# First keys on ScalarE's DMA queue, and a new order of two batches' normalisations in block 0 of a cross-attention and FFN kernel

## The chip, the cores and the metric

The kernel runs on one NeuronCore of one Trainium2 chip. The metric is the device time of one execution in microseconds (us). A core has five instruction streams that run beside each other and meet only through semaphores: TensorE (PE, matrix products; its weight loads are listed as PEld), VectorE (DVE), ScalarE (ACT), GpSimd (POOL) and SyncE (SP), which here only issues DMAs. ACT and POOL can issue DMAs as well. Each stream handles its instructions in the order of the program.

## The reference

Eight sequences of 256 tokens with 256 features go through one block. LayerNorm here has no learned parameters.

```python
x = x + softmax(mask(layernorm(x) @ ctx.T / 16)) @ ctx      # causal and key padding masks
h = silu((layernorm(x) @ w1.T) * w1_s) * ((layernorm(x) @ w2.T) * w2_s)
h = gelu((h @ h1.T) * h1_s)                                 # 1024 x 1024, ternary weights
h = gelu((h @ h2.T) * h2_s)
x = x + (h @ w3.T) * w3_s
```

## The kernel before

Two sequences make a block (`NB` = 2, 512 tokens, four tiles of 128 tokens), and there are four blocks, worked on in two pairs. For a pair, `pair` runs the FFN; its two wide layers use sums and differences of operand blocks in place of some products, and nearly all of the matmuls are there (L824). Operands are split into a high and a low part (`hyt` and `lyt`, `oh` and `ol`). The attention of later blocks is put between the FFN's steps by a plan written by hand (`stages_at`). The order of every engine's instructions is that in which the Python code emits them; no scheduler reorders them.

Only the attention of **block 0** runs with nothing beside it, as the prologue of the kernel. It is cut into two groups of one sequence each (`groups(0)` is `((0,), (1,))`), here called the first and the second batch; tiles 0 and 1 belong to the first, 2 and 3 to the second. `attention` holds one generator `stages` per batch and lets each go to its next `yield` in turn, so the two batches alternate stage by stage:

- `load_block` (L109) issues the DMAs. For block 0: mi, the mask row, on ACT's queue (L120); x as four tiles on SP (L123); the keys kt of the first and of the second batch on SP (L126); the values vs on SP (L129). Behind these SP issues the scales sc and s3 (L186, L188).
- Warm-up matmuls on zeros follow on PE (`keep_warm`, L161), then constants on POOL, and a load of ACT's square-root table (L184).
- `queries_turned` (L405), first stage: `sums` (L257) issues for each tile of the batch a statistics instruction (L261) and an aggregate (L262) on DVE. After the first batch's, DVE makes the mask row `row16` (L411). `masks_first` puts the masks into the score banks with bf16 matmuls (L370, L377); the L377 matmuls read `row16`.
- Second stage: `normed` (L278) issues the square root on ACT (L269, `root`), the reciprocal on DVE (L275, `turned_over`), and for each tile one `tensor_scalar` on DVE (L283, `scaled`) that gives the normalised tile of `ya`. Behind the second batch's, POOL copies one column (L419, `passed`), which holds back the weight loads behind it on POOL's queue (L148) until x is through.
- Third stage: four transposes for each batch on PE (`turned`, L301, tiles `pqt`), copied as `qt` by ACT for the first batch (L426) and by DVE for the second (L428). ACT then loads its exponential table (L339).
- Scores on PE (`ps`, L470), row maxima on DVE (L492), exponentials on ACT (L500), transposes (`pp`, L513), copies and reciprocals on DVE (L517 to L524), values on PE (`pv`, L537).
- The residual sum: one `scalar_tensor_tensor` on DVE for each tile (L551), which writes the tile of x again. For the first batch its accumulator gives the sums from which ACT makes the second LayerNorm's centre and root (L566 to L576). For the second batch `sums` follows. The list `held` carries a closure, `begun` (L578), from the first batch to the second's `sums`: it issues the first batch's reciprocal on DVE (L580) and the scaling of its tile 0 on POOL (L584). Tile 1 is scaled by DVE afterwards.
- Then, for the second batch, root, table load for the FFN's Silu (L339), reciprocal and two scalings; on PE the transposes of x (`pxt`), five warm-up matmuls (L161), and the transposes of `yf` (`pyt`). DVE casts the first batch's result and half of the second's to the high part `hyt` (L608), ACT casts the other half (L610), DVE makes the low part (L313). The first FFN matmuls are at L890.

Of the kernel before, what the change touches and what calls it, by code (L numbers as in the profile page):

```python
# [43 lines left out]
P = 128  # L44
B, S, D, H = 8, 256, 256, 1024
NB = 2
NT = NB * S // P
# [27 lines left out]
def _network(ctx, tc, g, exact, flag):  # L75
    nc = tc.nc
# [19 lines left out]
    def new(p, shape, tag, name, dt=F32, **kw):  # L96
        return p.tile(shape, dt, tag=tag, name=f"{v}{name}", **kw)

    def groups(t):

        return ((0,), (1,)) if t == 0 else ((0, 1),)

    def tokens(js):
        return slice(js[0] * S, (js[-1] + 1) * S)

    def tiles(js):
        return slice(2 * js[0], 2 * js[-1] + 2)

    def load_block(t, behind=None):  # L109

        xs = new(io, [P, NT, D], "xs", f"xs_{t}", bufs=2)
        kt = new(io, [P, NB, ND, S], "kt", f"kt_{t}", bufs=2)
        vs = new(io, [P, NT, D], "vs", f"vs_{t}", bufs=2)
        mi = new(io, [P if t else 1, TB], "mi", f"mi_{t}", I32)
        span = bass.ts(t, TB)
        if behind is not None:
            for tile_ in (xs[:, 0, :1], kt[:, 0, 0, :1], vs[:, 0, :1], mi[:, :1]):
                behind.memset(tile_, 0)
        if t == 0:
            nc.scalar.dma_start(out=mi, in_=g.mask[:, span])  # L120
        step = NT if t else 1
        for i in range(0, NT, step):
            nc.sync.dma_start(out=xs[:, i : i + step, :], in_=g.x[t, :, i : i + step, :])  # L123
        for n, js in enumerate(groups(t)):
            own = slice(js[0], js[-1] + 1)
            nc.sync.dma_start(out=kt[:, own], in_=g.ctx_t[t, :, own])  # L126
            if n == 0 and t:
                nc.sync.dma_start(out=mi, in_=g.mask[:, span].to_broadcast([P, TB]))
        nc.sync.dma_start(out=vs, in_=g.ctx_n[t])  # L129
        return xs, kt, vs, mi  # L130
# [11 lines left out]
    def load_weight(w, name):  # L142
# [7 lines left out]
        return chunks  # L150

    loaded = {0: load_block(0)}

    zeros = None if exact else new(work, [P, 2 * RAW], "raw", "zeros", BF16, bufs=3)
# [99 lines left out]
        yield  # L254
        yield nc.values_load(flag[0:1, 0:1], min_val=0, max_val=P * (LOW + len(wide) * RAW))

    def sums(src, js, mv, name, between=()):  # L257

        stats = new(tiny, [P, NT, nc.vector.BN_STATS_DIM], "stats", f"st{name}", bufs=2)
        for i in range(NT)[tiles(js)]:  # L260
            nc.vector.bn_stats(out=stats[:, i, :], in_=src[:, i, :])  # L261
            nc.vector.bn_aggr(out=mv[:, :, i], in_=stats[:, i, :])  # L262
            while between:
                between.pop()()

    def root(js, mv, name):
        own = tiles(js)
        std = new(tiny, [P, NT], "std", f"sd{name}", bufs=2)
        nc.scalar.activation(std[:, own], mv[:, 1, own], AF.Sqrt, bias=eps)  # L269
        return std  # L270

    def turned_over(js, std, name):
        own = tiles(js)
        rstd = new(tiny, [P, NT], "rstd", f"rs{name}", bufs=2)
        nc.vector.reciprocal(rstd[:, own], std[:, own])  # L275
        return rstd

    def normed(src, js, mv, y, name):  # L278
        scaled(src, range(NT)[tiles(js)], mv, turned_over(js, root(js, mv, name), name), y)

    def scaled(src, own, mv, rstd, y, engine=nc.vector):
        for i in own:
            engine.tensor_scalar(  # L283
                y[:, i, :],
                src[:, i, :],
                mv[:, 0, i : i + 1],
                rstd[:, i : i + 1],
                ALU.subtract,
                ALU.mult,
            )  # L290
# [45 lines left out]
    def table(t, js, func):  # L336

        if t == 0 and js == groups(t)[0 if func == AF.Exp else -1]:
            nc.scalar.activation(junk, eps, func)  # L339
# [65 lines left out]
    def queries_turned(t, js, once, xs, mi, pss):  # L405

        cols = tokens(js)
        mva = once("mva", "mva", [P, nc.vector.BN_AGGR_DIM, NT], tiny, bufs=2)
        sums(xs, js, mva, f"a_{t}_{js[0]}")
        if t == 0 and js == groups(t)[0]:  # L410
            nc.vector.tensor_scalar(row16[:, :TB], mi, 0.0, NEG, ALU.is_equal, ALU.mult)  # L411
        if not t:
            masks_first(js, pss)
        yield
        y = once("y", "ya", [P, NT, D])
        normed(xs, js, mva, y, f"a_{t}_{js[0]}")
        if t == 0 and js == groups(t)[-1]:
            passed = new(const, [P, 1], "passed", "passed")
            nc.gpsimd.tensor_copy(passed, y[:, NT - 1, :1])  # L419
        yield  # L420
        bias = mask_bias(t, js, once, mi)
        qt = once("qt", "qt", [P, ND, TB])
        for c, pt in turned(y, js, f"pqt_{t}_{js[0]}", *(() if t else (ps_mm, "mm"))):

            if t or js == groups(t)[0]:
                nc.scalar.activation(qt[:, c, cols], pt, AF.Copy, scale=1.0 / 16.0)  # L426
            else:
                nc.vector.tensor_scalar(qt[:, c, cols], pt, 1.0 / 16.0, None, ALU.mult)  # L428
        table(t, js, AF.Exp)
        yield  # L430
        return qt, bias, None
# [25 lines left out]
    def stages(t, js, once, result, xs, kt, vs, mi):  # L457
# [62 lines left out]
        own = slice(js[0], js[-1] + 1)  # L520
# [5 lines left out]
        for j in js:  # L526
            if t:
                pv = ps_at.tile([P, 2, D], F32, tag="at", name=f"{v}pv_{t}_{j}")
                pvs = [pv[:, h, :] for h in range(2)]
            else:  # L530

                p, tag = (ps_at, "at") if j else (ps_mm, "mm")
                pvs = [p.tile([P, D], F32, tag=tag, name=f"{v}pv_0_{j}_{h}") for h in range(2)]
            for h, (a, e) in enumerate(SPANS):
                n = (e - a) // P
                for k in range(n):
                    nc.tensor.matmul(  # L537
                        pvs[h],
                        lhsT=prt[:, j, bass.ds(a + k * P, P)],
                        rhs=vs[:, 2 * j + k, :],  # L540
                        start=(k == 0),
                        stop=(k == n - 1),
                    )

            first_ = len(groups(t)) > 1 and js == groups(t)[0]
            if first_:
                total, centre, squares, std = (
                    new(const, [P, 2], n, n) for n in ("total", "centre", "squares", "std0")
                )
            for h in range(2):  # L550
                nc.vector.scalar_tensor_tensor(  # L551
                    xs[:, 2 * j + h, :],
                    pvs[h],
                    rden[:, j, h : h + 1],
                    xs[:, 2 * j + h, :],
                    ALU.mult,
                    ALU.add,
                    **(dict(accum_out=total[:, h : h + 1]) if first_ else {}),
                )
        if t:  # L560
            yield
        mvf = once("mvf", "mvf", [P, nc.vector.BN_AGGR_DIM, NT], tiny)
        if first_:
            y = once("y", "yf", [P, NT, D])
            for i in range(2):
                nc.scalar.activation(  # L566
                    centre[:, i : i + 1], total[:, i : i + 1], AF.Copy, scale=-1.0 / D
                )
                nc.scalar.activation(
                    y[:, i, :],  # L570
                    xs[:, i, :],
                    AF.Square,
                    bias=centre[:, i : i + 1],
                    accum_out=squares[:, i : i + 1],
                )
            nc.scalar.activation(std, squares, AF.Sqrt, bias=eps, scale=1.0 / D)  # L576

            def begun():  # L578

                nc.vector.reciprocal(std, std)  # L580
                shifted(0, nc.gpsimd)

            def shifted(i, engine):
                engine.tensor_scalar(  # L584
                    y[:, i, :],
                    xs[:, i, :],
                    centre[:, i : i + 1],
                    std[:, i : i + 1],
                    ALU.add,
                    ALU.mult,  # L590
                )

            held.append(begun)
        else:
            sums(xs, js, mvf, f"f_{t}_{js[0]}", held)
        yield
        xst = once("xst", "xst", [P, ND, TB])
        yt = []
# [27 lines left out]
        if near(t):  # L626
            y = once("y", "yf", [P, NT, D])
# [19 lines left out]
        else:  # L647
# [5 lines left out]
            mean, rstd = on_all(mvf, ("row", "row2"), f"mf_{t}")  # L653
# [3 lines left out]
            y = once("y", "yf", [P, ND, TB])  # L657
# [600 lines left out]
```

## Time and profile before

| What | Value |
|---|---|
| Median of three timed runs | 349.14 us (347.75 to 349.73) |
| The profiled execution | 347.43 us |
| Its span, first to last instruction | 345.6 us |
| Mean granted TensorE clock | 0.995 |
| x's first tile, DMA issue to landing (chain) | 0.73 to 3.15 us |
| DVE's first statistics | 3.18 us |
| First score matmul (ps) | 7.84 us |
| First FFN matmul (L890) | 18.69 us |
| x (512 KB in four), keys (512 KB in two), values (512 KB) of block 0 | all issued by SP, 0.73 to 3.97 us |

The profile is that of one execution. A busy share says how long an engine had an instruction in hand. The chain that ended last is followed back from the last instruction: at each step to what released it, or to the instruction before it on its engine. A group in the timeline or the chain has its start, its duration, the engine, the line of the code, and how many instructions were merged; what stands in brackets is the time that the engine had been idle before it and what ended that.

### The profile page before, as it was taken

The page shows a single profiled execution, that of the slowest core. Times are in us where ns is not written, and L with a number is a line of the kernel's source. Part 1 is how long each engine was busy: PE and PEld are TensorE (multiplying, and loading weights), DVE is VectorE, ACT ScalarE, POOL GpSimd, SP SyncE. Part 2 cuts the span into 40 slices and gives each one's busy share as a digit, 9 for nine tenths or more (in the row PEclk, how much of TensorE's full clock was granted, in tenths as well). Part 3 has the DMA queues.
Part 4 walks back from the last instruction along what each step waited for, and adds up shares of the span by engine and source line. Part 5 has one row for each costly group of instructions (what it writes and reads, how often), then busy time and mean ns, then how long its engine had stood idle before and what let it go on. Part 6 is the DMA issues. An engine that isn't in the chain of part 4 may idle for free.

```text
span 345.6 us, 4329 instructions
## 1 busy us (share of the span) xinstructions
PE 334.0 (97%) x1508; PEld 269.9 (78%) x1508; DVE 270.3 (78%) x411; ACT 216.4 (63%) x301; POOL 36.6 (11%) x78
## 2 busy tenths in 40 slices
PE   8999999999999999999999999999999999999991
PEld 4777887877888888887888788886788887888781
DVE  5779876999799848686997875889948987856761
ACT  4866833358855854858671675356896686767620
POOL 3610000210002300030000003000010000000000
PEclk9999999999999999999999999999999999999998
DMA  5999972997596642579517474960635579530032
GB/s 184 342 297 273 294 256 82 358 280 252 151 399 228 197 146 99 164 251 326 204 47 246 127 251 127 292 248 2 243 123 182 173 250 353 201 121 0 0 123 70
DMA packets 20702, 68.81 MB, mean 199 GB/s; under 512 B 2465, under 2 KB 5313, under 8 KB 17090
## 3 DMA queue, kind: packets, MB, share of 16 engines
q0 software_dynamic: 7488, 36.70, 33.0%
q1 hardware_dynamic: 13040, 31.63, 27.2%
q8 instruction: 14, 0.23, 0.3%
q14 instruction: 14, 0.11, 0.1%
q10 hardware_dynamic: 146, 0.13, 0.1%
HBM read 55.86 MB, written 8.40 MB: 186 GB/s over the span
## 4 chain that ended last, share of the span: by engine, by line
PE 79%; DVE 8%; DMA 5%; ACT 3%; issue 2%; POOL 1%; DVEq 0%; POOLq 0%; ACTq 0%; SPq 0%
PE px_u L824 29%; PE px_y L824 15%; PE po L1112 8%; PE p L824 7%; PE pa L684 5%; PE pb L684 5%; PE ps L470 3%; PE pv L537 3%; DMA raw<-h2q 3%; DMA raw<-h1q 1%; DVE sign L218 1%; DVE ol L313 1%; PE pqt L301 1%; ACT oh L807 1%; DVE sta L261 1%
## 5 line engine op out<-in xcount | busy, mean ns | idle before, releaser
L824 PE MATMUL px_u<-oh,a 128*128 128x512 f32 x256 | 71.7, 395 | 1.1 <-ACT oh L807 0.8
L824 PE MATMUL px_u<-ol,a 128*128 128x512 f32 x256 | 70.8, 391 | 0.0
L824 PEld LDWEIGHTS px_u<-ol,a 128*128 128x128 f32 x256 | 47.9, 188 | 11.6 <-DVE ol L313 1.5
L824 PEld LDWEIGHTS px_u<-oh,a 128*128 128x128 f32 x256 | 47.5, 188 | 11.8 <-ACT oh L807 1.2
L697 ACT ACTIVATE gate<-pa,sc 128x512 f32<-128x512 f32 x32 | 21.6, 686 | 24.5 <-PE pa L684 22.1
L824 PE MATMUL px_y<-oh,a 128*128 128x512 f32 x128 | 34.5, 391 | 0.0
L824 PE MATMUL px_y<-ol,a 128*128 128x512 f32 x128 | 34.2, 389 | 0.0
L824 PEld LDWEIGHTS px_y<-ol,a 128*128 128x128 f32 x128 | 24.0, 188 | 5.0
L824 PEld LDWEIGHTS px_y<-oh,a 128*128 128x128 f32 x128 | 23.9, 188 | 5.0
L216 ACT ACTIVATE sign<-raw 128x1024 bf16<-128x1024 f32 x16 | 16.9, 1055 | 9.5 <-DMA raw<-h2q 4.1
L768 POOL DMA_DIRECT2D a<-S x16 | 8.5, 534 | 131.6 <-PE px_u L824 55.5
L218 DVE SCALAR_TENSOR_TENSOR sign<-raw,sign 128x1024 bf16<-128x1024 f32 x16 | 19.3, 1219 | 2.7 <-ACT sign L216 2.7
L684 PE MATMUL pa<-hyt,w 128*128 128x512 f32 x60 | 19.1, 399 | 0.2 <-DVE na L855 0.2
L684 PE MATMUL pb<-hyt,w 128*128 128x512 f32 x60 | 18.6, 391 | 0.2 <-DVE res L711 0.2
L684 PE MATMUL pa<-lyt,w 128*128 128x512 f32 x60 | 18.5, 390 | 0.0
L684 PE MATMUL pb<-lyt,w 128*128 128x512 f32 x60 | 18.5, 389 | 0.0
L852 ACT ACTIVATE nd<-nd,sc 128x512 f32<-128x512 f32 x16 | 10.7, 715 | 11.7 <-DVE nd L855 11.7
L824 PE MATMUL p<-oh,a 128*128 128x512 f32 x64 | 17.4, 394 | 0.4 <-DVE na L855 0.4
L313 DVE TENSOR_TENSOR ol<-nT,oh 128x1024 fp32r<-128x1024 f32 x12 | 14.5, 1222 | 3.6 <-ACT oh L807 3.6
L824 PE MATMUL p<-ol,a 128*128 128x512 f32 x64 | 17.1, 389 | 0.0
L855 DVE TENSOR_TENSOR na<-p,na 128x512 f32<-128x512 f32 x16 | 10.9, 688 | 7.9 <-PE p L824 7.9
L852 ACT ACTIVATE nb<-nb,sc 128x512 f32<-128x512 f32 x16 | 10.7, 717 | 10.0 <-DVE nb L855 10.0
(196 smaller groups left out, 651.1 us busy)
## 6 DMA issues: line engine op xcount, KB each, us to landing
a<-S POOLq DMA_DIRECT2D x16, 1024.0 KB, 5.1
a<-h1q POOLq DMA_DIRECT2D x6, 1024.0 KB, 7.8
a<-h2q POOLq DMA_DIRECT2D x6, 1024.0 KB, 5.1
raw<-h1q SPq DMA_DIRECT2D x8, 512.0 KB, 4.3
raw<-h2q SPq DMA_DIRECT2D x8, 512.0 KB, 5.9
vs<-ctx_n SPq DMA_DIRECT2D x4, 512.0 KB, 7.5
q<-h1q POOLq DMA_DIRECT2D x4, 512.0 KB, 20.1
q<-h2q POOLq DMA_DIRECT2D x8, 256.0 KB, 14.0
```

What stands on the lines that cost most here:

```text
L216: nc.scalar.activation(sign, raw, AF.Sign)
L218: nc.vector.scalar_tensor_tensor(sign, raw, 1.0, sign, ALU.mult, ALU.not_equal, accum_out=count[:, n : n + 1])
L313: nc.vector.tensor_tensor(lo, value, hi.bitcast(F32), ALU.subtract)
L470: nc.tensor.matmul(pss[j][h], lhsT=qt[:, c, bass.ts(2 * j + h, P)], rhs=kt[:, j, c, : e - a], start=(c == 0 and t > 0), stop=(c == ND - 1) ...
L537: nc.tensor.matmul(pvs[h], lhsT=prt[:, j, bass.ds(a + k * P, P)], rhs=vs[:, 2 * j + k, :], start=(k == 0), stop=(k == n - 1),)
L684: nc.tensor.matmul(pm, lhsT=wc[:, bass.ts(o, P)], rhs=x, start=(n == 0), stop=(n == len(steps) - 1),)
L697: nc.scalar.activation(gate, pa, AF.Silu, scale=sc[:, 0, o : o + 1])
L768: nc.gpsimd.dma_start(out=a, in_=src)
L824: nc.tensor.matmul(bank, lhsT=a[:, k, bass.ts(o, P)], rhs=x[k // 2][part][:, k % 2, :], start=start and (part, k) == steps[0], stop=stop a ...
L852: nc.scalar.activation(out, src, AF.Gelu, scale=sc[:, n, o : o + 1])
L855: nc.vector.tensor_tensor(out, one, other, ALU.add)
L1112: nc.tensor.matmul(po, lhsT=w3[j * QK + k][:, bass.ts(o, P)], rhs=xs_[j][k // 2][part][:, k % 2, :], start=(j == 0 and (part, k) == STEPS[0]),
```

## The change

Three edits, which touch block 0 and the functions that it shares with block 1. Nothing is computed differently, apart from one scaling that another engine does.

1. The first batch's keys are issued on ACT's DMA queue behind mi, instead of on SP's behind x.
2. The first batch's first normalisation is put into the closure list `held`, and the second batch's `sums` runs it ahead of the statistics of tile 3. Its tile 0 is scaled by POOL, its tile 1 by DVE.
3. `sums` takes a function `ahead`, called before each tile's statistics, and it now runs the closures in `held` before the second tile's statistics instead of after the first tile's aggregate. For the second batch the residual sums of x (L551) are no longer issued both at once but one ahead of each tile's statistics.

For block 1, whose `sums` call of the first normalisation now also gets `held`, that list is empty. The instructions on DVE change their order, not their number; the same goes for SP but for one DMA that moves to ACT, and POOL has one scaling more, DVE one less, in block 0.

```diff
             own = slice(js[0], js[-1] + 1)
-            nc.sync.dma_start(out=kt[:, own], in_=g.ctx_t[t, :, own])
+            queue = nc.sync if t or n else nc.scalar
+            queue.dma_start(out=kt[:, own], in_=g.ctx_t[t, :, own])
...
-    def sums(src, js, mv, name, between=()):
+    def sums(src, js, mv, name, between=(), ahead=None):
         stats = new(tiny, [P, NT, nc.vector.BN_STATS_DIM], "stats", f"st{name}", bufs=2)
-        for i in range(NT)[tiles(js)]:
+        for n, i in enumerate(range(NT)[tiles(js)]):
+            if ahead is not None:
+                ahead(n)
+            while n and between:
+                between.pop()()
             nc.vector.bn_stats(out=stats[:, i, :], in_=src[:, i, :])
             nc.vector.bn_aggr(out=mv[:, :, i], in_=stats[:, i, :])
-            while between:
-                between.pop()()
...
-        sums(xs, js, mva, f"a_{t}_{js[0]}")
-        if t == 0 and js == groups(t)[0]:
+        sums(xs, js, mva, f"a_{t}_{js[0]}", held)
+        y = once("y", "ya", [P, NT, D])
+        very_first = t == 0 and js == groups(t)[0]
+        if very_first:
+            def begun():
+                rstd = turned_over(js, root(js, mva, "a_0_0"), "a_0_0")
+                scaled(xs, (0,), mva, rstd, y, nc.gpsimd)
+                scaled(xs, (1,), mva, rstd, y)
+            held.append(begun)
             nc.vector.tensor_scalar(row16[:, :TB], mi, 0.0, NEG, ALU.is_equal, ALU.mult)
         if not t:
             masks_first(js, pss)
         yield
-        y = once("y", "ya", [P, NT, D])
-        normed(xs, js, mva, y, f"a_{t}_{js[0]}")
+        if not very_first:
+            normed(xs, js, mva, y, f"a_{t}_{js[0]}")
...
-            for h in range(2):
+            def added(h, j=j, pvs=pvs):
                 nc.vector.scalar_tensor_tensor(
                     xs[:, 2 * j + h, :],
...
+            if t or first_:
+                added(0)
+                added(1)
...
-            sums(xs, js, mvf, f"f_{t}_{js[0]}", held)
+            sums(xs, js, mvf, f"f_{t}_{js[0]}", held, None if t else added)
```

## The prediction

> **What bounds the kernel now.** I read the page first, for who is busy and when.
>
> ```profile
> span 345.6 us, 4329 instructions
> PE 334.0 (97%) x1508; PEld 269.9 (78%) x1508; DVE 270.3 (78%) x411; ACT 216.4 (63%) x301; POOL 36.6 (11%) x78
> ```
>
> TensorE (PE) is busy for 334.0 of 345.6 us. Busy time by stretch shows where the missing 11.6 us lie: PE works for 16.34 of the first 18.6 us and for 317.66 of the last 327.0 (2.26 and 9.34 us idle). After 18.6 us matmuls run with short waits, and none of the edits is there: their instructions all belong to block 0's attention, which is over by 19 us, and the later waits shift along with the run. So the change can only move the moment at which the long run of matmuls begins, and whatever that moves goes through to the end one for one. The whole stake is the prologue, and of it only its serial chain. So I read the chain that ended last, cut to the first 32 us (start, duration, what).
>
> ```profile
> 0.73 2.42 DMA xs<-x
> ...
> 5.54 0.18 DVE mva L262
> ...
> 7.22 0.78 PE pqt L301 x4
> 8.00 2.74 PE ps L470 x16
> ...
> 12.28 2.61 PE pv L537 x12
> ...
> 16.57 0.29 ACT sdf L269
> ...
> 16.88 1.28 ACT L339
> ...
> 18.28 0.36 ACT hyt L610
> ...
> 18.69 0.76 PE pa L890 x2
> ```
>
> The reader is to see a relay without slack: x lands, VectorE (DVE) makes the statistics, PE transposes, scores run (ps), softmax, values (pv), the sums of the second batch, a square root, a table load on ScalarE (ACT), one cast, and the first FFN matmul at 18.69. The timeline adds what stands beside the relay.
>
> ```profile
> 4.38 0.30 ACT L269 ACTIVATE sda<-mva,eps 128x2 f32<-128x2 f32 x1 [1.60 <-DVE mva L262]
> ...
> 6.66 0.74 DVE L283 TENSOR_SCALAR ya<-xs,mva,rsa 128x256 f32<-128x256 f32 x2
> ...
> 15.94 1.24 PE L161 MATMUL warm<-zeros 128*128 128x512 bf16 x5
> 16.19 0.55 POOL L584 TENSOR_SCALAR yf<-xs,centre,std 128x256 f32<-128x256 f32 x1 [2.76 <-issue]
> 16.45 0.43 DVE L584 TENSOR_SCALAR yf<-xs,centre,std 128x256 f32<-128x256 f32 x1
> ...
> 17.02 1.42 PE L301 MATMUL pyt<-ident,yf 128*128 128x128 f32 x8
> ...
> 17.75 1.15 DVE L608 CAST hyt<-pyt 128x512 fp32r<-128x512 f32 x2
> ```
>
> **Part 1, first normalisation.** Nothing is removed; one of four L283 operations goes to GpSimd (POOL), and the first batch's reciprocal and its tile 1 go ahead of the statistics of tile 3. DVE's pitches, from the rows: 0.43 from statistics to aggregate, 0.10 to the next instruction, 0.17 from reciprocal to scaling, 0.33 from scaling on. Tile 2's aggregate starts at 5.02 as before; the square root is ready (4.38 + 0.30 = 4.68). So reciprocal 5.12, tile 1 at 5.29 to 5.70, statistics of tile 3 at 5.62 instead of 5.12, aggregate 6.05 to 6.23, ACT's root 6.27 to 6.56, second reciprocal 6.59, then (0.20 behind a reciprocal that waited, as at 16.90 to 17.10) tile 2 at 6.79 and tile 3 from 7.12 to 7.53. Before, tile 3 was done at 6.66 + 0.74 = 7.40. The **first batch gains**: POOL, 0.2 behind the reciprocal as at L584, takes 0.55 and ends at 6.0, four transposes need 0.84 (7.19 to 8.03), so ACT can copy at 6.9 instead of 7.19. The **second batch loses** 0.13.
>
> Which of them counts? PE issues in program order, and both batches' transposes stand ahead of the first score. Before, the first score started at 7.84, when both had just ended together: ACT's copy at 7.19 + 0.60 = 7.79, and the last transpose, issued some 0.3 after tile 3's scaling. With the change the copy is 0.3 early, the transposes 0.13 late: the score starts 0.13 late. The early copy brings the table load behind it forward, but the exponentials after the first wait for DVE's maxima, which wait for PE's scores. So this part costs **+0.13**, bounds 0 (the second reciprocal waits less than I take) and +0.3 (VectorE slowed beside GpSimd). Behind POOL's new instruction stand the marker copy (L419) and the weight loads; that copy waited for tile 3 already, so they move by the 0.13. W2 is needed only at about 19 us and landed 7.8 after an issue near 9.
>
> Does GpSimd beside VectorE cost? At L584 both scale tiles at once: 0.55 and 0.43, where L283 alone takes 0.41. I take 0.02. The Trainium skill's page "SBUF — State Buffer", section "Who interferes with whom", speaks against this: a GpSimd operation and a VectorE `tensor_scalar` in a 2-port mode hold a shared port pair exclusively, and the later one blocks entirely. By it VectorE at 16.45 would have stood until 16.74, which the row does not show. If it held in the new place, GpSimd would end at some 6.25; that is still ahead of the second batch, so the sum would be the same.
>
> **Part 2, keys on ACT's queue.** ACT's issue of mi takes 0.52 (0.73 to 1.25); the first keys follow for some 0.45, so ACT's table load (1.29, 1.28 long) ends near 3.0 instead of 2.57. It is hidden: the first root is wanted at 4.38. On SP the second keys, vs, sc and s3 go 0.45 earlier. Nobody waits for them: keys landed 3.7 after an issue at 2.59 to 3.05, before 7, and the score wants them at 7.84. So the move **gains nothing**. What it can lose is x. Until now SP issued four x tiles ahead of all keys, one per 0.45 (four in 1.81); tile 0 landed at 3.15, so tiles 1 to 3 by that pitch at 3.60, 4.05 and 4.50. From now on 256 KB of keys enter the same 16 engines with tile 1. Three answers of the DMA view, cut to 5 to 6.5, 14.8 to 16.0 and 17.8 to 19.8 us (queue: packets, MB, share of engines):
>
> ```profile
> q1 hardware_dynamic: 217, 0.51, 99.1%
> ```
> ```profile
> q1 hardware_dynamic: 58, 0.24, 53.0%
> q0 software_dynamic: 58, 0.22, 51.3%
> ```
> ```profile
> q0 software_dynamic: 67, 0.53, 65.9%
> q1 hardware_dynamic: 71, 0.29, 38.3%
> ```
>
> The first says that 16 full engines move 340 GB/s of such packets, so the keys take 256 / 340 = 0.77 us of all engines. The others say that two queues share by packets, not bytes: 58 to 58, 67 to 71, and the queue with the bigger packets gets more bytes. Keys have packets twice as long as x's 1 KB, so x gets a third while both are pending. From 2.0 to 4.4 the engines are 77% busy; in some 1.2 us of contention that leaves 0.28 free. Tile 1 is then late by 0.77 - 0.28, say 0.5: 4.10 instead of 3.60, and its statistics start at 4.13 instead of 3.74. That is **+0.4** on the relay. Later tiles have more slack: tile 2 at 4.55 is wanted at 4.96, tile 3 later still. Bounds: 0 (tile 1's packets all get in first), and 0.8 (tile 0 is hit by all of the keys' time too). No row shows ACT and SP loading together, so I take the middle, nearest to the shared-queue rows.
>
> **Part 3, second batch's x and statistics.** Before: add, add, statistics, aggregate, reciprocal, statistics, aggregate. Now the first statistics go between the adds. Pitches: add to next 0.40, statistics to aggregate 0.45, then 0.10. First add 14.05, statistics 14.45, aggregate 14.90, second add 15.00 instead of 14.91 (its pv ended at 14.88), first batch's reciprocal at 15.49 (ACT's std ends at 15.46) instead of 15.86, statistics 15.54 instead of 15.91, the root at 16.20 instead of 16.57. So **0.37 is won at the root**, and ACT's table load and its cast could follow. But the second add is 0.09 late; it feeds four transposes, behind which, in PE's order, stand five warm-up matmuls and then the yf transposes, which started at 17.02 straight after the last warm-up. They start at 17.11 now. Four of them (0.11 apart, the last 0.27 long) end at 17.71, and DVE's first cast, which had waited for DVE itself until 17.75, now waits for them until 17.75. Its two casts end at 18.43 and 18.90 as before. The first FFN matmul waits for the first of them and for ACT: 18.49 instead of 18.69; the second waits for the second cast, and its weights load at 18.95, as before. **What is late next is VectorE's casts**, and the gain ends there: 0, bounds -0.37 and +0.09.
>
> **Sum.** 0.13 + 0.4 + 0 = +0.53 us on a profiled run of 347.43 (345.6 of span): 347.96. That run is 1.71 under the median of the three timed runs, 349.14 (347.75 to 349.73); the difference goes onto the median: **349.7 us**, +0.15%. Under 0.5% (1.75 us) is about what a measurement of this kernel can't tell from no change, so I forecast **no change**.
>
> **The rivals.**
> - *The new order pays.* Keys slip past x, and Part 3 keeps its 0.37: 0.13 - 0.37 = -0.24, 348.9. For it: 23% of engine time is free while x loads. Against it: L608 has no slack, and warm-up matmuls stand before pyt.
> - *Keys hit x in full.* Tile 0 and tile 1 wait out the whole 0.77: 0.8 + 0.13 + 0.09 = +1.0, 350.2. For it: a transfer lands when its slowest engine does. Against it: the keys enter some 0.5 behind tile 0.
> - *Slower, by PE's pace.* The first warm-up matmuls are 0.43 apart (2.44, 2.87, 3.29), the five later ones some 0.22 (1.24 for five); the pace doubled by 4.67, just as the row-mask matmuls began. Those wait for DVE's L411, which part 2 makes 0.4 late. If that hole keeps PE slow for one more block of work, the scores cost their 2.74 twice: +2.74 + 0.53, 352.4. It decides from the hole being long enough to undo the warm-up. Against it: at 11.84 PE had sat idle for 0.63 before L513's transposes without slowing. The Trainium skill's "TensorE: Matmul & The Clock Gate", Part 1, puts the idle time needed at about 3.4 us; by it this rival is worth nothing.
> - *The change does nothing visible*: each edit hidden, 349.1. It is the forecast without contention, and I count it there.
>
> **How the numbers follow.** Forecast, hidden edits included, 0.60; the order pays 0.18; keys in full 0.14; pace 0.08. Single runs of the kernel before spread by 1 us either side, so a median of a few can stray by as much. Range: 348.9 - 1.0 = 347.9 to 350.2 + 1.0 = 351.2; the pace case and some straying stay outside. Slower by over 0.5% (above 350.9): the pace's 0.08, and straying from the forecast (0.09) and from keys in full (0.04): 0.21. Faster by over 0.5% (below 347.4): straying from the first rival and the forecast, 0.08. Between: 0.71.
>
> **What would show it.** In the profile after: tile 1's statistics waiting for x's DMA past 3.8; the first score at 8.2 to 8.5 (7.84 before), of which 0.13 remain if x is on time; the root some 0.37 earlier against pv's end than the 1.69 of before, and yet the second FFN matmul's weights no earlier against it. I am wrong if tile 1 is on time, if the L608 casts move forward with the root, or if matmuls of the scores are twice as far apart.

## The result and the profile after

| | before | after |
|---|---|---|
| Median of 22 runs each, taken in turns on one chip | 347.61 us (345.73 to 349.73) | 348.93 us (346.71 to 350.57) |
| Ratio, with its 95% interval | | 1.0053 (1.0036 to 1.0070) |
| The profiled execution, and its span | 347.43, 345.6 | 349.05, 347.2 |
| Statistics of tile 1, of tile 2 start | 3.74, 4.57 | 5.29, 6.16 |
| First score matmul starts | 7.84 | 9.87 |
| The 16 score matmuls (ps) take | 2.89 | 4.15 |
| First weight load of the FFN | 18.69 | 21.90 |

The changed kernel is **slower**: by the ratio 1.84 us (1.25 to 2.43), or 0.53%, with an interval that leaves out no change; the two medians are 1.32 apart, which lies in that interval. The lines below, from the page of the changed kernel, show that TensorE (PE) has hardly more to do; the time is one of waiting and of pace.

```profile
span 347.2 us, 4330 instructions
PE 335.0 (96%) x1507; PEld 271.4 (78%) x1508; DVE 270.3 (78%) x410; ACT 216.8 (62%) x301; POOL 37.9 (11%) x79
```

The chain that ended last, cut to the first 32 us (start, duration, what):

```profile
1.18 4.09 DMA xs<-x
5.29 0.44 DVE sta L268
...
6.94 1.37 POOL ya L288
8.36 1.72 PE pqt L306 x8
10.08 3.96 PE ps L485 x16
...
19.59 0.29 ACT sdf L274
...
21.93 0.78 PE pa L910 x2
```

Before, this chain began with x's first tile (0.73, 2.42 long) and had the scores at 2.74. Now it begins with a **later tile of x, 4.09 us** on its way, goes over a GpSimd (POOL) scaling that was not there, and the same 16 score matmuls take 3.96. The timeline of the changed kernel (in brackets the idle time before, and what ended it) says who waited:

```profile
5.29 0.43 DVE L268 BATCH_NORM_STATS2 sta<-xs 128x6 f32<-128x256 f32 x1 [1.50 <-DMA xs<-x]
...
6.29 0.21 PE L382 MATMUL ps<-row 1*128 1x128 bf16 x1 [0.98 <-DVE row L426]
...
6.94 1.36 POOL L288 TENSOR_SCALAR ya<-xs,mva,rsa 128x256 f32<-128x256 f32 x1 [4.07 <-DVE rsa L280]
```

VectorE (DVE) stood 1.50 us for x; behind it the mask row was late, and PE stood 0.98 us before its row-mask matmuls.

**Where the 3.21 us at the FFN's start come from** (21.90 - 18.69), by these rows: 1.59 are there when tile 2's statistics start; 0.44 more come up to the first score (9.87 against 7.84 is 2.03), where GpSimd's scaling lies; the scores take 1.26 longer; and the rest of the way is 0.08 shorter. **Where they go:** the profiled spans differ by 1.6 only. The stretch behind the FFN's start is 325.3 us long here and 326.9 before. Over the twelve profiles of the experiments it is 325.5 to 326.8, in no order by the size of the prologue, so it has a scatter of its own of some 1.5 us, and these two profiles lie at its ends. A small part of it can be named. In the chain of the kernel before, cut to 277 to 296 us, stands a DMA; behind it and two steps on ACT, PE stood idle for 0.30 us, up to 290.72:

```profile
279.39 9.23 DMA raw<-h2q
```

The rest stays open. In the same cut, the chain of the changed kernel has matmuls alone:

```profile
276.95 19.27 PE px_u L844 x85
```

So the timed ratio, not the two spans, is the measure of the change.

### The profile page after: what moved, and what is told of

Same layout as the page of the kernel before. It is cut to its first block, busy times and chain, and to the rows that moved or that the text cites. A ratio compares the mean times of both kernels' runs of the same rounds, so it can differ in the third digit from the quotient of the medians.

```text
span 347.2 us, 4330 instructions
## 1 busy us (share of the span) xinstructions
PE 335.0 (96%) x1507; PEld 271.4 (78%) x1508; DVE 270.3 (78%) x410; ACT 216.8 (62%) x301; POOL 37.9 (11%) x79
## 4 chain that ended last, share of the span: by engine, by line
PE 84%; DVE 7%; ACT 3%; DMA 2%; issue 2%; POOL 1%; SPq 0%; POOLq 0%; DVEq 0%; ACTq 0%
PE px_u L844 34%; PE px_y L844 15%; PE po L1132 8%; PE p L844 7%; PE pa L704 5%; PE pb L704 5%; PE ps L485 3%; PE pv L552 3%; DMA raw<-h1q 1%; DMA xs<-x 1%; DVE ol L318 1%; PE pqt L306 1%; PE pxt L306 1%; PE pp L528 1%; DVE sta L268 1%
```

## The experiments

The first theory after the result was that the keys on ScalarE's (ACT's) queue cost x's tiles their time on the DMA engines (K where a letter stands for it). Its rivals were edit 2 (GpSimd's scaling and the new order), edit 3, and PE's clock by itself; later came the question why GpSimd's scaling took 1.36 us, with its first use of such an instruction (F) as one answer.

| Run | Tile 1's statistics | First score | Scores take | FFN starts | Ratio to before |
|---|---|---|---|---|---|
| after | 5.29 | 9.87 | 4.15 | 21.90 | 1.0053 (1.0036 to 1.0070) |
| e1_keys | 4.81 | 9.52 | 4.70 | 22.25 | 1.0073 (1.0046 to 1.0099) |
| e2_nokeys | 3.76 | 8.13 | 2.89 | 18.90 | 1.0010 (0.9984 to 1.0037) |
| e3_adds | 3.77 | 7.90 | 2.89 | 18.67 | 1.0008 (0.9988 to 1.0028) |
| e4_norm | 3.71 | 8.12 | 2.89 | 18.97 | 1.0014 (0.9990 to 1.0037) |
| e5_dve | 3.70 | 8.28 | 2.79 | 18.93 | 1.0023 (1.0001 to 1.0046) |
| e6_first | 3.76 | 8.16 | 2.89 | 18.93 | 1.0019 (0.9992 to 1.0045) |
| e7_late | 3.74 | 8.98 | 3.36 | 20.21 | 1.0019 (0.9991 to 1.0047) |
| e8_warm | 4.49 | 9.17 | 2.89 | 19.93 | 1.0035 (1.0013 to 1.0057) |
| e9_half | 3.79 | 8.85 | 3.84 | 20.65 | 1.0025 (0.9991 to 1.0060) |
| e10_best | 3.73 | 7.86 | 2.89 | 18.43 | 0.9998 (0.9973 to 1.0023) |
| e11_add | 3.78 | 8.38 | 4.13 | 20.39 | one run, 347.82 us |
| e12_none | 3.71 | 7.95 | 2.89 | 18.52 | 0.9991 (0.9971 to 1.0011) |

The middle columns are of one profiled execution each, the ratio of several runs.

**e1_keys**: the kernel before with edit 1 alone.

```diff
-            nc.sync.dma_start(out=kt[:, own], in_=g.ctx_t[t, :, own])
+            queue = nc.sync if t or n else nc.scalar
+            queue.dma_start(out=kt[:, own], in_=g.ctx_t[t, :, own])
```

> Only the keys' move to ACT's queue, all else as before. Theory K (the keys share the DMA engines with x's tile 1): tile 1's statistics start at about 5.3 us instead of 3.74, as in the changed kernel, the first FFN weights load about 1.5 us later than before's 18.69 (20.2; up to 21.5 if PE's clock is also cut), and the time rises by some 1.3 us (0.4%). Theory G (GpSimd's slow scaling, 1.36 us in the changed kernel, is what costs): FFN start 18.7 to 18.9, time within 0.1% of before.

Measured: tile 1 at 4.81, the scores at 4.70, and 1.0073, as much as the whole change or more. The first edit by itself gives the loss.

**e2_nokeys**: the changed kernel without edit 1.

```diff
-            queue = nc.sync if t or n else nc.scalar
+            queue = nc.sync
```

> The changed kernel with the keys back on SP's queue. Theory K: tile 1's statistics at 3.7 again, GpSimd's scaling costs at most some 0.5 us at the first score (it started at 7.84 before), FFN start 18.8 to 19.3, time within 0.15% of before. Theory G: the scaling still takes 1.36 us and the FFN starts at 20 us or later, time +1 us (0.3%) or more. Theory C (PE waits long enough for its clock to be cut, whatever makes it wait): scores take 2.74 us here, since PE's wait is short.

Measured: tile 1 at 3.76 and the scores at 2.89, as before; 1.0010, an interval that holds 1. Taken out, edit 1 takes the loss with it. What remains is the first score 0.29 late, and a part of its cause stands in the timeline of this run (e5 below tells how much):

```profile
5.38 1.35 POOL L288 TENSOR_SCALAR ya<-xs,mva,rsa 128x256 f32<-128x256 f32 x1 [2.51 <-DVE rsa L280]
```

**e3_adds** and **e4_norm**: e2 with edit 3 alone (the first normalisation as in the kernel before), and with edit 2 alone. The diff is e4's:

```diff
-            if t or first_:
-                added(0)
-                added(1)
+            added(0)
+            added(1)
...
-            sums(xs, js, mvf, f"f_{t}_{js[0]}", held, None if t else added)
+            sums(xs, js, mvf, f"f_{t}_{js[0]}", held)
```

> Only the third edit: the second batch's residual sums tile by tile. By the step of the prediction the gain at the root is lost again at VectorE's casts, which wait for the transposes behind the warm-up matmuls: root about 0.37 us earlier against the end of pv, FFN's second weight load no earlier, time within 0.1% of before. Rival (the new order pays): FFN start 18.3, time -0.1%.

> Only the second edit: the first batch's normalisation between the second's statistics, its tile 0 on GpSimd. By the prediction's step (GpSimd 0.55 us): first score at 8.0 instead of 7.84, FFN start 18.8. By what the changed kernel showed (GpSimd 1.36 us): transposes from 6.8 us, first score at about 8.3, FFN start 19.2, time +0.1%. If GpSimd needs 0.55 us here, its 1.36 us came from what stood beside it (late x, DMAs) and not from its place as the first operation of its kind.

Measured: neither can be told from the kernel before by its time. In the profiles edit 2 puts the first score at 8.12 (7.84 before). Edit 3 brings the root forward to 1.43 behind the last value matmul (16.36 - 14.93; 1.70 before, 16.57 - 14.87), and yet the FFN's start moves by only 0.02. Its timeline shows why:

```profile
16.19 1.24 PE L163 MATMUL warm<-zeros 128*128 128x512 bf16 x5
...
17.27 1.04 PE L306 MATMUL pyt<-ident,yf 128*128 128x128 f32 x8
...
17.91 1.02 DVE L618 CAST hyt<-pyt 128x512 fp32r<-128x512 f32 x2 [0.28 <-PE pyt L306]
```

VectorE is free 0.28 earlier than its first cast starts and waits for the yf transposes, which stand behind the five warm-up matmuls. The first of the two casts ends at 18.60, and the FFN's first weights follow at 18.67.

**e10_best** and **e12_none**: edit 3 alone, with two and with none of these five warm-up matmuls (the diff is e10's; e12 has 9, 0).

```diff
-WARM, WARM_LATER = 9, 5
+WARM, WARM_LATER = 9, 2
```

> Only the third edit, with two instead of five warm-up matmuls between the transposes of x and of yf. The step of the prediction (the gain at the root is lost behind the warm-up matmuls): with three fewer of 0.22 us each, the yf transposes start at 16.5 to 16.6 us instead of 17.1, VectorE's first cast at 17.4 to 17.5 instead of 17.75 to 17.91, FFN start 18.3 to 18.4 instead of 18.67, time 0 to 0.15% under before. Rival (something else holds the casts): FFN start 18.6 or later.

> Only the third edit, with no warm-up matmuls between the transposes of x and of yf. The casts then wait for VectorE's scalings alone: VectorE's first cast at 17.4, FFN start 18.3 as with two. Theory C at its edge: PE has idle time here between 16 and 17 us; if its clock is cut for that, the first FFN matmuls are 0.45 us apart instead of 0.23 and the time rises by 0.3% or more; if not, the time is 0 to 0.15% under before.

Measured, in e10's timeline:

```profile
16.58 1.60 PE L306 MATMUL pyt<-ident,yf 128*128 128x128 f32 x8
...
17.49 1.15 DVE L618 CAST hyt<-pyt 128x512 fp32r<-128x512 f32 x2
```

The transposes start 0.69 earlier than in e3, the cast 0.42, the FFN's weights 0.24. So the warm-up matmuls were the bound that ate edit 3's gain. Without any of them the FFN starts at 18.52, no better than with two, and PE's clock was not cut. Neither ratio leaves 1 out: **no version beats the kernel before** by more than can be told.

**e5_dve**: e2 with the new scaling given back to VectorE.

```diff
-                scaled(xs, (0,), mva, rstd, y, nc.gpsimd)
+                scaled(xs, (0,), mva, rstd, y)
```

> The changed kernel with the keys on SP's queue and tile 0 scaled by VectorE instead of GpSimd. By VectorE's pitches: reciprocal 5.13, tiles 0 and 1 at 5.30 and 5.63, statistics of tile 3 at 5.96, tile 3's scaling done at about 7.9, first score at 8.25 to 8.4 us (8.13 with GpSimd, 7.84 before), FFN start 19.0 to 19.2, time within 0.2% of before. If the first score is at 8.0 or earlier, GpSimd's half only cost.

Measured: the first score at 8.28 and the FFN at 18.93, where e2 has 8.13 and 18.90, with 1.0023 against 1.0010. GpSimd's half gains nothing that can be told, and what edit 2 loses isn't GpSimd's alone: with VectorE the second batch's scalings end at 7.83 and the score follows 0.45 behind them; with GpSimd they end at 7.58, but all eight transposes (1.34 to the first score) start only at 6.79, behind GpSimd's tile (6.73) and the last mask matmul (6.79). In e6 below, the masks end earlier, at 6.14, and PE stands 0.68 us for GpSimd alone.

**e6_first**: e2, with a small scaling of the same kind on GpSimd ahead of all, to pay for a first use early.

```diff
+    tried = new(const, [P, 16], "tried", "tried")
+    nc.gpsimd.tensor_scalar(tried, causal[:, :16], eps, eps256, ALU.subtract, ALU.mult)
```

> The changed kernel with the keys on SP's queue, and with one small scaling of the same kind (128x16) put on GpSimd's queue ahead, right behind its constants. Theory F (the first operation of a kind on GpSimd takes some 0.8 us more): the small one takes about 0.9 us, tile 0's scaling falls from 1.36 to 0.55 us, transposes start at 6.1 us instead of 6.8, first score at 8.0, FFN start 18.7 to 18.8, time within 0.15% of before. Rival (VectorE beside it holds GpSimd up): tile 0's scaling still takes about 1.36 us.

```profile
2.87 0.42 POOL L186 TENSOR_SCALAR tried<-causal,eps,eps 128x16 f32<-128x16 f32 x1
...
5.40 1.36 POOL L290 TENSOR_SCALAR ya<-xs,mva,rsa 128x256 f32<-128x256 f32 x1 [2.11 <-DVE rsa L282]
```

The second operation took 1.36 us, as without the small one ahead of it: **the theory of the first use falls**. By the two rows one element of the free axis costs (1.36 - 0.42) / 240 = 3.9 ns, an estimate: most of the cost goes with the size.

**e11_add**: e2, with GpSimd's scaling as add and multiply, the pair of operations of the 0.55 us row in the second LayerNorm, in place of subtract and multiply.

```diff
-                scaled(xs, (0,), mva, rstd, y, nc.gpsimd)
+                scaled(xs, (0,), mva, rstd, y, nc.gpsimd, ALU.add)
```

> The changed kernel with the keys on SP's queue, GpSimd's first scaling with add and multiply instead of subtract and multiply; it adds the mean where the reference subtracts it, so it is read for its time alone. Theory S (subtract is the slow operation on GpSimd; the later scaling at L604 adds and needs 0.55 us, and the 16-column try needed 0.42): tile 0's scaling falls from 1.36 to about 0.55 us, transposes start at 6.1 to 6.3 us, first score at about 8.0. Rival (its place beside VectorE's statistics makes it slow): still about 1.36 us.

```profile
5.44 0.68 POOL L288 TENSOR_SCALAR ya<-xs,mva,rsa 128x256 f32<-128x256 f32 x1 [2.56 <-DVE rsa L280]
```

Half of 1.36: the pair of operations explains most of the gap to 0.55; 0.13 stay open. The first batch's transposes started at 6.17, right behind GpSimd's end at 6.12, and the copy on ACT moved from 7.48 to 6.87, but in this one execution PE's clock was cut (below), so its later times say nothing on edit 2.

**e7_late**: the changed kernel, the keys on ACT's queue but issued behind ACT's first table load and the activation after it.

```diff
-            queue = nc.sync if t or n else nc.scalar
-            queue.dma_start(out=kt[:, own], in_=g.ctx_t[t, :, own])
+            if t or n:
+                nc.sync.dma_start(out=kt[:, own], in_=g.ctx_t[t, :, own])
...
+    nc.scalar.dma_start(out=loaded[0][1][:, :1], in_=g.ctx_t[0, :, :1])
```

> The changed kernel with the first keys still on ACT's queue, but issued behind ACT's table load and its first activation, about 2.8 us instead of 1.3. Theory K (sharing of the DMA engines while x lands): tile 1's statistics at about 3.75 again, FFN start about 18.95 as in the run with keys on SP, time within 0.2% of before. Rival (ACT's queue itself is slow or disturbs SP's): tile 1's statistics past 4.5 us and a time 0.3% or more above before.

Measured: tile 1 back at 3.74, and 1.0019, where the changed kernel has 1.0053 (the two intervals overlap). Tile 1's delay depends on **when** the keys enter the engines (issued at 3.15 us here, at 1.28 in the changed kernel), not on the queue that carries them, as the theory of the keys has it; by the times alone this isn't shown. The forecast of the later stages missed: the first score is at 8.98 and the FFN at 20.21. In this execution PE had its full pace only from 9.99 us, although x was on time and PE had no gap up to 7.2 (more on this under e8).

**e9_half**: the kernel before, half of the first keys on ACT's queue, so that their packets have 1 KB instead of 2.

```diff
-            nc.sync.dma_start(out=kt[:, own], in_=g.ctx_t[t, :, own])
...
+                for c, queue in enumerate((nc.scalar, nc.sync)):
+                    queue.dma_start(out=kt[:, own, c], in_=g.ctx_t[t, :, own, c])
```

> The kernel before with only half of the first keys (128 KB in packets of 1 KB) on ACT's queue behind mi, the other half on SP behind x. Theory K, by bytes and packets: tile 1's statistics between 3.9 and 4.4 us (3.74 before, 4.81 with all the first keys there), FFN start 19 to 19.7 if PE's clock holds, time +0.1 to +0.4%. Rival (a second hardware queue delays x whatever it carries): tile 1 as late as with all the keys, 4.8 us or more.

Measured: tile 1 on time (3.79), tile 2 late instead (5.25; 4.57 before); 1.0025, with an interval (0.9991 to 1.0060) that holds no loss as well as the change's whole loss, so the time decides nothing here. The DMA view between 2.4 and 3.9 us (queue: packets, MB, share of the 16 engines) of the kernel before, of the changed kernel and of e9, where q1 is SyncE's queue and q10 ACT's:

```profile
q1 hardware_dynamic: 415, 0.38, 76.8%
```
```profile
q10 hardware_dynamic: 83, 0.16, 57.3%
q1 hardware_dynamic: 167, 0.15, 32.4%
```
```profile
q1 hardware_dynamic: 353, 0.32, 67.6%
q10 hardware_dynamic: 136, 0.12, 25.5%
```

Before, x had the engines alone and moved 0.38 MB. In the changed kernel the engines are busier (89.7%) and move less, 0.31 MB, of which x gets half. A packet's mean time is its queue's share x 16 x 1.5 us over the count: x's 44 ns before and 47 after, the keys' **166 ns** (189 in e1). Read packet by packet in the traces, that mean has two parts. The keys' 2 KB packets took 84 ns by the median, in the changed kernel as in the kernel before; but 15 of 78 in this stretch took between 0.25 and 0.88 us and hold 8.0 of the 13.7 us. In e9 the keys' 1 KB packets on ACT's queue take 45 ns and the sum is 0.45 MB.

A second queue isn't needed for such slow packets. With all keys on SyncE's queue, e2 has 13 of them between 2.4 and 5.4 us, up to 0.73 us long, and between 3.9 and 5.4 it moves 0.36 MB with the engines 90.2% busy; x is all but through by then, and nobody waits. So what edit 1 did was to put the keys' slow packets **beside x's**. What makes them slow stays open, and so does what helped in e9, which halved the packets' length and the bytes on ACT's queue at once.

**e8_warm**: the changed kernel, with matmuls on zeros put into PE's gap: two more at the start, four behind the mask matmuls.

```diff
-WARM, WARM_LATER = 9, 5
+WARM, WARM_LATER = 11, 5
...
             masks_first(js, pss)
+            keep_warm(4 * (js[0] == 1))
```

> The changed kernel with two more warm-up matmuls at the start and four more behind the mask matmuls, so that PE has work while x is late. Theory C (PE's idle time is what cuts its clock): full clock from about 6 us on, the sixteen score matmuls in 2.7 to 2.8 us instead of 4.15, FFN start about 20.6, time about 1.2 us (0.35%) under the changed kernel's and still above before's by 0.2 to 0.4%. Rival (the clock is cut for another reason): scores still take about 4 us, time as the changed kernel's or longer.

Measured: the scores at 2.89 again and 1.0035. Stretches of 3.41 us of the changed kernel (stretch, length, busy time of PE, PEld, DVE, ACT and POOL with counts, granted PE clock, DMA share, GB/s):

```profile
5.83:9.25 3.42, 2.28 (x13) 1.18 (x12) 2.80 (x11) 0.79 (x3) 1.40 (x2) 1.00 0.47 173
9.25:12.66 3.41, 3.41 (x14) 3.01 (x14) 0.98 (x2) 2.34 (x5) 3.40 (x11) 0.50 0.58 167
```

The granted clock is **0.50 for one such stretch**, which holds the scores. In the one ahead of it PE was busy for 2.28 of 3.42 us. The corresponding stretch of the kernel before and of e8:

```profile
4.32:7.73 3.41, 3.28 (x19) 1.62 (x16) 2.93 (x12) 1.13 (x3) 0.27 (x2) 1.00 0.83 283
```
```profile
5.19:8.60 3.41, 3.41 (x21) 1.75 (x18) 2.73 (x10) 0.66 (x3) 1.40 (x2) 1.00 0.59 200
```

Both were followed by a full clock. In e9 and e11 a stretch with PE busy for 2.60 and 2.79 of 3.41 us was followed by a clock of 0.50, too.

The mean granted clock of each timed execution says how often this happens. It is 0.992 or less in 12 of the 22 executions of the changed kernel (0.990 in the profiled one) and in 4 of the 8 of e1, but in none of the 12 of e8, in none of the 95 of the kernel before in the experiments, and in 7 of the 84 of e2, e3, e4, e5, e6, e10 and e12, whose keys are all on SyncE's queue. (At 0.993 it can be either: e9's profile has a cut at that mean. The kernel before has 0.993 nine times, e8 twice.) So with the keys moved the cut comes in at least half of the executions, and the filled gap takes it nearly or wholly away: it was the gap and not the late x as such.

The cut isn't the only way to a slow start. In e1's profile PE had half its pace from the beginning to about 13.3 us:

```profile
6.46:9.88 3.42, 3.42 (x14) 2.33 (x14) 2.09 (x9) 1.29 (x3) 1.31 (x3) 1.00 0.28 97
9.88:13.29 3.41, 3.41 (x13) 3.05 (x13) 1.25 (x3) 1.90 (x5) 3.41 (x12) 1.00 1.01 335
```

The clock column's 1.00 says nothing here: no clock is on record ahead of its first change, and the column then shows 1.00, as it does for the slow warm-up matmuls of every run. The matmuls themselves tell: 13 in the second stretch, as few as in the changed kernel's cut one (14). PE was busy for all of the first stretch, and yet the second ran at half pace; e7's clock came late with x on time. Why it rose late in these two stays open.

What the pace costs in time stays open, too. The 12 executions of the changed kernel with the low mean clock have a median of 348.93 us, the other ten 348.87; a clock that rises late isn't in that mean (0.995 in e1's profile). And e8's tile 1 came at 4.49, 0.8 earlier than in the changed kernel's profile with the same DMAs, so only part of its gain of 1.97 at the FFN's start is the clock's; and the timed ratios, 1.0035 and 1.0053, overlap.

## Why the prediction was right and wrong

It said no change, 349.7 us, +0.53 on the kernel before. The measured 348.93 lies in its range, but that is partly luck, and the base helped: the kernel before had 349.14 in the three runs shown and 347.61 in the 22. The difference is what was forecast, and by the ratio it is **+1.84 instead of +0.53** (+1.32 by the medians): at the edge of the 0.5% that the forecast called no change, and by the ratio just beyond it, on the side to which it gave 0.21. Of its three signs of being wrong, the last came: in the profile the score matmuls were twice as far apart for most of their time.

- **Only the start can move things, one for one.** The place was right: every delay that the profiles show is in the prologue. "One for one" can't be read from one pair of profiles: the FFN's start moved by 3.21 and the span by 1.6, since the stretch behind it scatters by 1.5 us. Nor do the timed differences have to equal one profile's: 2.5 us in e1 (0.73%) against 3.56 there.
- **Part 2, the keys at +0.4: the step that failed.** It took "256 / 340 = 0.77 us of all engines" and sharing "by packets". The 340 GB/s came from a stretch in which the 2 KB packets took 84 ns each and longer ones were among them (217 packets for 0.51 MB); the keys' 128 packets at the measured mean of 166 ns are 1.33 us of 16 engines, since some of them were slow. Nor did the queues share by packets: 83 to 167, which is equal bytes. The equal counts of the other two rows belonged to a software queue beside a hardware queue. Tile 1 came 1.55 late. In e1 and e8, with the same keys on ACT's queue, it came 1.07 and 0.75 late, so two of three profiles lie beyond the upper bound of 0.8, which rested on the same 340 GB/s. What was right: nobody waits for the keys, so the edit gains nothing; x's second tile is hit; the relay has no slack there.
- **The rival of PE's pace** was given 0.08 and came in together with the keys; the mechanism (late x, late mask row, a hole in PE's work, scores at half pace) was the one that was written down, at +1.26 in place of 2.74, because the cut lasted one stretch of 3.41 us that also held other work. Nor was it an unlikely case: the cut came in at least half of the executions. "The hole being long enough to undo the warm-up" was tested against a single idle gap (0.63 without effect); the longest gaps here were 0.98 and 0.69. The Trainium skill's "TensorE: Matmul & The Clock Gate", Part 1, asks for about 3.4 us of idle time. The measurement differs, and it decides: here a stretch of that length with PE busy for two thirds of it was enough. What share is needed stays open: 2.79 of 3.41 was cut in e11, 3.28 was not before, and 2.70 was not in e6 (4.01 to 7.42), so busy time is not all that counts; and where the clock's stretches begin differs from execution to execution (5.83 us in the changed kernel's profile, 4.17 in e9's, 4.30 in e11's).
- **Part 1 at +0.13** measured 0.29 and 0.28 (e2, e4). The second batch went as written: last scaling done at 7.58 in e2, 7.53 predicted. That POOL "takes 0.55" failed: 1.35, mostly because the 0.55 row multiplies behind an add, and this one behind a subtract (0.68 with an add in e11). So the first batch's copy on ACT, put at 6.9, came at 7.48, and the eight transposes, which the working had begun early, ran in one row up to the first score. By the 0.45 that e5 shows behind the last scaling, the score would else have come at 8.03: by this estimate GpSimd costs 0.10 of the 0.29, the order the rest. In the changed kernel 0.44 stand in this place; the remaining 0.15 or so lie in the transposes, which ran past 9.25 into the cut clock (1.57 from GpSimd's end to the first score, 1.40 in e2). VectorE wasn't held up beside GpSimd: at L604 of the changed kernel it began second (19.47; GpSimd 19.17 to 19.72) and took 0.40. Nor did GpSimd stand until VectorE was done: in e11 it began second (5.44; VectorE 5.36 to 5.77) and took 0.68, only 0.13 over that 0.55. The lock between the two that the Trainium skill's "SBUF — State Buffer", "Who interferes with whom", describes for VectorE's 2-port modes does not show here; whether VectorE ran in such a mode, no run shows.
- **Part 3 at 0: right, with its reason.** The root came 0.27 earlier (0.37 predicted; the statistics started 0.52 behind the add that they read, not 0.40) and the FFN no earlier; the casts wait for the transposes behind the warm-up matmuls (e3), and move once some of these are gone (e10). This is the step that the diff alone would have led one to count as a gain.

## What to carry to other kernels

A load that nobody waits for can still cost, if it enters the DMA engines beside one that is waited for: keep it behind, in the same queue or by a later issue, and price it by a row that holds its own packets beside the others', not by a steady stretch. A short stall ahead of TensorE can be paid twice where it thins PE's work enough to lower the clock for the stretch that follows; look at the granted clock stretch by stretch and at the spacing of the matmuls, not at the longest gap, and over many executions, not one. Before counting an earlier result as a gain, look for what stands ahead of its consumer in the consumer's own order.

## What the runs showed of the hardware that was not expected

- GpSimd's fp32 `tensor_scalar` of 128x256 took 1.36 us with subtract and multiply, 0.68 and 0.55 with add and multiply; VectorE's takes 0.41.
- TensorE's granted clock fell to 0.50 for 3.41 us after a stretch of that length with PE busy for 2.28, 2.60 or 2.79 us of it; no gap of PE in the changed kernel's stretch was over 0.98 us.
- In e1 TensorE stayed at half pace through a stretch of 3.41 us that followed one in which PE was busy for all of 3.42 us.
- Some 2 KB packets of the keys took 0.25 to 0.88 us where the median is 84 ns: 15 of 78 beside x's 1 KB packets on another queue, with the sum down from 253 to 207 GB/s, and 13 in e2, on one queue. With 1 KB packets on both queues (e9) they took 45 ns in the mean, and the sum was 297 GB/s.
